# A graph network's convolution loop: ten products with a zero matrix in each group of edges

## Chip, cores and metric

One core of a Trainium2 chip runs the whole kernel in one launch. The metric is the device time of that launch in microseconds (us); ten runs of the kernel before give a median of 4104.05 us (4099.78 to 4107.27).

TensorE (PE in the profile) does the matrix products, VectorE (DVE) and ScalarE (ACT) the elementwise work, GpSimd (POOL) issues the indirect gathers, SyncE (SP) the plain transfers. PEld is TensorE's loading of the stationary matrix, which overlaps its products. "Granted clock" is the share of TensorE's full clock that the throttle let through.

## What is computed

Two graph layers on 6250 nodes of 128 features and 200000 edges sorted by destination. The first (graph attention, two passes) fills the first half of the time and is not touched. The second is a convolution over edges, and the change lies in its loop:

```python
h = jnp.maximum(_layernorm(x), 0.0)
f0, f1 = x0 @ W_lin0_feat, einsum('nui,uv->nvi', x1, W_lin1_feat)   # of h, per node
e0, e1 = f0[edge_src], f1[edge_src]                                  # gathered per edge
a0, a1 = edge_attr[:, 0], edge_attr[:, 1:4]
h = gelu(gelu(edge_scalar_attr @ W_mlp1) @ W_mlp2)                   # 8 -> 64 -> 64 per edge
w = einsum('pxu,ex->epu', W_tp, h)                                   # 4 x 32 weights per edge
m0 = w[:, 0] * e0 * a0
m1 = w[:, 3] * einsum('eui,ei->eu', e1, a1)
m2 = w[:, 1] * e0 * a1
m3 = w[:, 2] * e1 * a0
agg = zeros.at[edge_dst].add(concat(m0, m1, m2, m3))                 # 256 sums per node
out = COS_MIX * self_part + SIN_MIX * (agg @ Wf)
x = x + out
```

(The constant scales are left out here.)

## The kernel before

**Tiles and groups.** The 200000 edges are 1563 tiles of 128 edges (an edge per partition). The loop over `groups` in the convolution takes eight tiles at a time (`SB` = 8): 196 groups, the last one of three tiles. Destinations are sorted, so 24 consecutive tiles (`CT` = 24, three groups) fall on a window of 128 nodes; these three groups are a *chunk*, and 66 chunks make up the loop. I call three consecutive groups a *cycle*.

**One open sum per chunk.** `state["acc"]` is a PSUM tile of 128 nodes x 512 columns (256 sums, each as a high and a low half in fp32r). It is `whole()`, a pool with one buffer. For each tile `scatter` (L1552) multiplies a one-hot matrix of destinations (`ohr`) by the messages (`halves`), 128 x 512, and adds it to that sum. `sink` (L1590 to L1601) says which matmul starts and which stops the accumulation: tile 0 and tile 23 of a chunk. At tile 6 it also adds what of the preceding chunk lies in this one's nodes (L1600). When a new chunk begins, `close` (L1582) copies the sum out on ACT, and `finish3` turns it into output rows in two steps, which are handed over to the two groups after it (`todo`): first transposes of the copy (L1560, eight matmuls) and a copy `at` (L1562), then products with the output weights (L1565, L1566) and the copy `o` (L1568).

**Work of a group, spread over three groups ahead.** While the messages of group g are made, the gather (L351, eight indirect DMAs on POOL) fetches the source rows of group g+1 into one of six `G` buffers, and ACT scales them into `g0` (L1494, eight activations). `layers(g+3)` is a generator with four steps for the edge network of group g+3: first matmul (L1475, from `a8t`), first GELU (L1478), second matmul (L1475, from `hid`), second GELU (L1478). Both of its matmuls write the one PSUM buffer `layer`. `weigh` (L1487) makes the weights `w` of group g+2 in a `big()` buffer, of which there are two.

**Messages on DVE** (`messages`, L1497 to L1542): L1507, L1509 and L1511 read the gathered `G`; then come the two halves of the `mess` part: L1518, L1519, a cast on ACT (L1527, L1532) and the residual of that cast (L1524); L1535 the other part, cast on ACT by L1537, with its residual L1541. L1541 is the last reader of the `big` buffer. L1545 makes the one-hots of the next group.

**Order.** `keep` fixes the order of each engine's instructions as the program writes them. On TensorE, a group issues: first matmul of g+3; a step of `finish3` if one is due, and then the second matmul at once; `weigh` of g+2; the second matmul if no step was due; the eight matmuls of `scatter`. On ACT: L1527, L1532, L1537; the second GELU if it was not yet issued (`between`); eight times L1494; the first GELU; `at` or `o`, or at a chunk's first group the copy of `close`; the second GELU at once if a step of `finish3` was due. So in a cycle there are three kinds of group:

- the *closing* group (the first of a chunk), which copies the old sum; its second GELU comes late, behind the next L1537 on ACT;
- the *transposing* group after it, whose first matmul has to wait for that late GELU (both use `layer`), and which then issues L1560;
- the *output* group, which issues L1565 and L1566.

In the transposing and the output group the second GELU stands in front of the next group's L1527 on ACT.

Of the kernel before, what the change touches and what calls it, by code (L numbers as in the profile page):

```python
# [32 lines left out]
BF16 = mybir.dt.bfloat16  # L33
# [10 lines left out]
P = 128  # L44
# [4 lines left out]
WSTEP = 16  # L49
HS = 7  # L50
CT, LT = 24, 40
DENSE1 = 20
LAG_D, AFTER, AFTER_D = 14, 12, 5
GP, GK, GSB = 125, 16, 4
# [9 lines left out]
def gnn_kernel(ctx: ExitStack, tc: tile.TileContext, x, src, dst, attr4, attr8,  # L64
# [3 lines left out]
    nc = tc.nc  # L68
# [24 lines left out]
    NT = src_t.shape[1]  # L93
    NG = NB - DENSE1
    HALF = P // 2
# [16 lines left out]
    keep = tc.keep_in_program_order  # L112

    def big():
        return ps_big.tile([P, 8, P], F32, tag="big", name="big")
# [10 lines left out]
    def whole():  # L126
        return ps_acc.tile([P, 512], F32, tag="acc", name="whole")
# [391 lines left out]
    def flags(pool, *why):  # L519

        flag = pool.tile([1, NB + 1], F32, name="flag")
        nc.vector.tensor_copy(flag[:, :NB], why[0])
        for w in why[1:]:
            nc.vector.tensor_tensor(flag[:, :NB], flag[:, :NB], w, op=OP.max)
        nc.vector.tensor_reduce(flag[:, NB:], flag[:, :NB], axis=AX.X, op=OP.max)
        flag_i = pool.tile([1, NB + 1], I32, name="flag_i")
        nc.vector.tensor_copy(flag_i, flag)
        return flag_i[:, :NB], flag_i[:, NB:]
# [146 lines left out]
    keep = lambda ins: ins  # L675
# [79 lines left out]
    rhs1 = [dram.tile([P, NB, HW], BF16, name=f"rhs1{q}") for q in range(H1 // 2)]  # L755
    deg1 = pool.tile([P, DENSE1], F32, name="deg1")

# [185 lines left out]
    def miscounted(pool, deg, edges, n):  # L943


        many = pool.tile([P, n], F32, name=f"many{n}")
        nc.vector.tensor_scalar(many, deg, 256.0, None, op0=OP.is_gt)
        ps = small()
        nc.tensor.matmul(ps[:1, :n], ones, deg, start=True, stop=True)
        nc.tensor.matmul(ps[:1, P:P + n], ones, many, start=True, stop=True)  # L950
        miss = pool.tile([1, n], F32, name=f"miss{n}")
        nc.vector.tensor_tensor(miss, ps[:1, :n], edges, op=OP.subtract)
        nc.vector.tensor_tensor(miss, miss, ps[:1, P:P + n], op=OP.subtract)
        nc.vector.tensor_scalar(miss, miss, -0.5, None, op0=OP.is_lt)
        return miss

    HH = H1 // 2 * C1
    assert DENSE1 % 4 == 0
    passes = [(b0, q) for b0 in range(NG, NB, 4) for q in range(H1 // 2)]
# [173 lines left out]
    def chunk_of(g):  # L1133
        return (g * SB + HT // 2) // HT

    def first_of(c):
        return max(0, HT * c - HT // 2)

    def last_of(c):
        return HT * c + HT // 2  # L1140
# [13 lines left out]
    def scatter(g, tiles):  # L1154
        c = chunk_of(g)
        if tiles[0] == 0 and g * SB == first_of(c):
            kept1["acc"] = whole()[:, :2 * (HD + H1)]
        for t in tiles:
            nc.tensor.matmul(kept1["acc"], ohs[g][:, t, :], mss[g][:, t].rearrange("e s f -> e (s f)"),  # L1159
                             start=g * SB + t == first_of(c), stop=g * SB + t + 1 == last_of(c))  # L1160
# [36 lines left out]
    for now in range(NGR * MS + MS):  # L1197
# [35 lines left out]
        if g and m >= 2:  # L1233
            scatter(g - 1, ((0, 1), (2, 3), (4,), (5,), (6,), (7,))[m - 2])
# [12 lines left out]
    keep = plain  # L1247
    nc.vector.tensor_scalar(wtp_sb[:, 0:3, :], wtp_sb[:, 0:3, :], 1.0 / math.sqrt(HID), None, op0=OP.mult)
    nc.vector.tensor_scalar(wtp_sb[:, 3, :], wtp_sb[:, 3, :], 1.0 / math.sqrt(3.0 * HID), None, op0=OP.mult)
    written_order.close()  # L1250
    nc.vector.tensor_tensor(over1[:, NG:], over1[:, NG:], miscounted(pool, deg1, n_edges[:, NG:], DENSE1), op=OP.max)
    again, some = flags(pool, over1, wide1.to_broadcast([1, NB]))
# [58 lines left out]
    with tc.tile_pool(name="att2", bufs=1) as pool, tc.tile_pool(name="dense", bufs=2) as dense, \  # L1311
# [68 lines left out]
        for b0 in range(0, NB, 2):  # L1380
            n = min(2, NB - b0)
# [10 lines left out]
            acc = big().rearrange("p (k a) c -> p k (a c)", k=2)  # L1392
            if b0 == 8:
                load_tiles(pool)
            for h0 in range(0, NB, HS):
# [15 lines left out]
                for j, made in ((0, up), (1, down)):  # L1411
                    for h in range(HS):
                        for k in range(n):
                            nc.tensor.matmul(acc[:, k, j * C2:(j + 1) * C2], made[:, h, k * P:(k + 1) * P],
                                             rhs2[:, h0 + h, j, :],
                                             start=h0 + h + j == 0, stop=h0 + h + j == NB)
                next(behind, None)
            parts = dense.tile([P, 2, 2, R2], F32, name="parts")
            acc = acc[:, :n, :2 * C2].rearrange("p k (j c) -> p k j c", j=2)
# [30 lines left out]
    cw = ctx.enter_context(tc.tile_pool(name="cw", bufs=2))  # L1450
# [31 lines left out]
    def weigh(n, hid, pw):  # L1482

        for j in range(min(n, NPR)):
            for c in range(j, n, NPR):
                half = slice(c // NPR * HID, (c // NPR + 1) * HID)
                keep(nc.tensor.matmul(pw[:, c, :], hid[half, j * P:(j + 1) * P],  # L1487
                           wtp_sb[half].rearrange("x p u -> x (p u)"), start=True, stop=True))
        return pw
# [54 lines left out]
    def one_hot3(dl, n, oh):  # L1544
        keep(nc.vector.tensor_tensor(oh[:, :n, :], slot[:, None, :].to_broadcast([P, n, P]),  # L1545
                          dl[:, :, None].to_broadcast([P, n, P]), op=OP.is_equal))
        return oh

    def scatter(ms, oh, cs, sink):
        for c in cs:  # L1550
            acc, start, stop = sink(c)
            keep(nc.tensor.matmul(acc, oh[:, c, :], ms[:, c].rearrange("e s h i u -> e (s h i u)"), start=start, stop=stop))  # L1552
# [19 lines left out]
    with tc.tile_pool(name="conv", bufs=1) as pool, tc.tile_pool(name="gath3", bufs=6) as gath:  # L1572
# [4 lines left out]
        state, todo = {}, deque()  # L1577

        def close(c):

            a = cw.tile([P, 2, 2 * D], F32, name="acc3")
            keep(nc.scalar.copy(a.rearrange("p s f -> p (s f)"), state["acc"]))  # L1582
            state["sums"] = [a[:, j] for j in range(2)]
            xb = cw.tile([P, D], F32, name="xb")
            nc.sync.dma_start(xb, xtd[ds(first_node(c), P), :])
            ending = finish3(state["sums"], xb, out[ds(first_node(c), P), :])
            next(ending)
            todo.extend([ending, ending])

        def sink(t):  # L1590
            c, k = divmod(t, CT)
            end = min(CT, NT - c * CT) - 1
            if k == 0:
                state["acc"] = whole()
            if k == min(6, end) and c:

                same = cw.tile([P, P], F32, name="same")
                keep(nc.vector.tensor_scalar(same, slot, shift[:, c - 1:c], None, op0=OP.is_equal))
                for a in state["sums"]:
                    keep(nc.tensor.matmul(state["acc"][:, :2 * D], same, a, start=False, stop=False))  # L1600
            return state["acc"], k == 0, k == end  # L1601

        groups = [(t, min(SB, NT - t)) for t in range(0, NT, SB)]

        def hots(g):
            t, n = groups[g]
            return one_hot3(dstc[:, t:t + n], n, cw.tile([P, SB, P], F32R, name="ohr", bufs=3))

        def layers(g):
            if g >= len(groups):  # L1610
                return iter(())
            t, n = groups[g]
            a8t = cw.tile([2 * NRAD, NPR * P], F32, name="a8t", bufs=4)
            for j in range(2 if n > NPR else 1):
                c = (t + j * NPR) * P
                nc.sync.dma_start(a8t[j * NRAD:(j + 1) * NRAD, :], attr8_t[:, c:c + NPR * P])
            return hidden(n, a8t)
# [8 lines left out]
        def keep_a1(t):  # L1626
            m = min(LT, NT - t)
            a1s = kept[:, P + t // LT % 2 * 3 * LT:P + (t // LT % 2 + 1) * 3 * LT].rearrange("p (k f) -> p k f", f=3)
            keep(nc.vector.tensor_copy(a1s[:, :m], a4s[t][:, :m, 1:]))
            return a1s  # L1630

        def fetch(g):
            t, n = groups[g]
            if t % LT == 0 and t + LT < NT:
                load_a4(t + LT)
            G = gath.tile([P, SB, D], F32, tag="G", name="G")
            gather(G, table3, srcc[:, t:t + n], n)
            return G, scaled(G, n, a4s[t // LT * LT][:, t % LT:t % LT + n, 0:1])
# [13 lines left out]
        for g, (t, n) in enumerate(groups):  # L1652
            G, g0 = rows
            i = t % LT
            last = g + 1 == len(groups)
            ms, after = messages(G, g0, n, a1s[:, i:i + n, :], pws.popleft(), None if last else lambda: hots(g + 1),
                                 lambda: hids.extend(list(second)[-1:]))
            if i + SB == LT and t + SB < NT:
                a1s = keep_a1(t + SB)
            first = layers(g + 3)  # L1660
            next(first, None)
            if not last:
                rows = fetch(g + 1)
            next(first, None)
            pw = big() if hids or todo else None
            if todo:
                todo.popleft().send(pw)
                next(first, None)
            if t and t % CT == 0:
                close(t // CT - 1)  # L1670
            if hids:
                pws.append(weigh(groups[g + 2][1], hids.popleft(), pw))
            next(first, None)
            scatter(ms, oh, range(n), lambda c: sink(t + c))
            second = first
            oh = after
# [118 lines left out]
```

## Time and profile before

| | |
|---|---|
| median of ten runs | 4104.05 us |
| the profiled execution | 4104.88 us, its span 4103.1 us |
| first and last gather of the convolution | 2125.2 us, 4078.9 us |
| TensorE busy in 2125 to 4075 us | 1481.63 of 1950 us, granted clock 0.84 |
| DVE busy there | 1746.55 us |
| ACT busy there | 1145.92 us |
| POOL busy there | 1474.56 us |
| mean granted clock of the whole span | 0.815 |

The convolution takes the second half of the span. A busy share does not tell which engine sets the pace: POOL's share counts only the gathers themselves, not the time between two of them in which it issues the next; TensorE's includes stretches at half clock. What ends each wait, in order of time, has to be read from the waits and the timeline.

### The profile page before, as it was taken

How to read it: one execution, taken by the hardware profiler on the slowest of the kernel's cores; microseconds unless marked ns; L12 is line 12 of the kernel's file. 1: busy time of each engine (PE TensorE's matmuls, PEld its weight loads, DVE VectorE, ACT ScalarE, POOL GpSimd, SP SyncE). 2: the span in 40 equal slices, each digit the busy share in tenths (PEclk: the TensorE clock that was granted, in tenths of full speed). 3: DMA queues.
4: the chain of work that ended last, by engine and by line, in shares of the span. 5: the costliest groups of instructions: out<-in, count | busy, mean ns of one | idle time of the engine just before them, and what ended most of it. 6: DMA issues, size and time to landing. Idle time of an engine off the chain costs nothing. (4 is left out here: it accounts for less than half of the span.)

```text
span 4103.1 us, 61327 instructions
## 1 busy us (share of the span) xinstructions
PE 2975.8 (73%) x19231; PEld 2091.8 (51%) x19232; DVE 3590.2 (87%) x6074; ACT 2793.1 (68%) x6317; POOL 2648.8 (65%) x2568
## 2 busy tenths in 40 slices
PE   3456676666666766999977777777777777777777
PEld 3344454444444546888854444444444444444444
DVE  6888988998988877899969989999998898988997
ACT  3458878887877776999965655655555555555555
POOL 5778877777877770000027777777777777777775
PEclk7557868887877777999978888888888888888888
DMA  4456656666666665544422222222222222222221
GB/s 120 146 166 186 192 166 178 190 185 180 179 176 174 183 171 189 182 163 168 166 70 61 63 62 63 62 63 63 62 63 62 64 62 62 63 62 63 62 62 49
DMA packets 391299, 482.40 MB, mean 118 GB/s; under 512 B 237609, under 2 KB 273300, under 8 KB 390950
## 3 DMA queue, kind: packets, MB, share of 16 engines
q1 hardware_dynamic: 307780, 332.00, 25.9%
q0 software_dynamic: 82400, 144.35, 13.5%
q8 instruction: 159, 2.61, 0.3%
q10 hardware_dynamic: 770, 1.88, 0.2%
q14 instruction: 190, 1.56, 0.1%
HBM read 374.52 MB, written 103.42 MB: 116 GB/s over the span
## 5 line engine op out<-in xcount | busy, mean ns | idle before, releaser
L351 POOL DMA_INDIRECT G<-table,srcc x1563 | 1478.3, 946 | 1019.4 <-DVE kept L1458 543.0
L351 POOL DMA_INDIRECT G<-table,srcw x936 | 1105.8, 1181 | 293.4 <-issue 270.3
L1095 ACT ACTIVATE up<-erb,sel 128x512 bf16<-128x512 f32 x980 | 689.4, 733 | 0.0
L877 PE MATMUL small<-key,lo 128*128 128x98 bf16 x3136 | 335.3, 241 | 256.7 <-ACT ca L859 233.0
L1552 PE MATMUL whole<-halves,ohr 128*128 128x512 f32 x1563 | 500.9, 458 | 0.7 <-ACT acc L1582 0.7
L1494 ACT ACTIVATE g<-G,a 128x128 f32<-128x128 f32 x1563 | 485.1, 393 | 12.4 <-DMA G<-table,srcc 9.8
L859 ACT CAST ca<-small 128x392 bf16<-128x392 f32 x784 | 381.0, 489 | 152.9 <-DMA counts<-ca 90.1
L1010 PE MATMUL up<-up,rc 128*102 128x512 bf16 x980 | 434.4, 464 | 47.7 <-DVE up L1019 23.2
L1401 ACT ACTIVATE ramp<-erb,sel 128x256 bf16<-128x256 f32 (+1 forms) x1138 | 458.3, 493 | 13.9 <-DVE up L1409 8.8
L1487 PEld LDWEIGHTS big<-wtp_sb,hid 64*128 64x128 f32 x3126 | 264.7, 250 | 370.7 <-issue 358.1
L877 PEld LDWEIGHTS <-lo 128*128 128x128 bf16 x3136 | 244.7, 117 | 366.1 <-issue 333.1
L1487 PE MATMUL big<-wtp_sb,hid 64*128 64x128 f32 x3126 | 306.5, 351 | 144.9 <-DVE halves L1541 144.4
L1552 PEld LDWEIGHTS whole<-halves,ohr 128*128 128x128 f32 x1563 | 313.3, 207 | 129.1 <-issue 53.9
L1159 PE MATMUL whole<-halves,ohr 128*128 128x136 f32 x936 | 365.2, 443 | 9.7 <-DVE ring L1167 9.7
L1478 ACT ACTIVATE hid<-layer 128x512 f32<-128x512 f32 x392 | 230.7, 589 | 198.9 <-PE layer L1475 198.9
L1475 PE MATMUL layer<-hid,wm_sb 128*128 128x512 f32 x392 | 347.7, 986 | 16.8 <-ACT hid L1478 15.0
L1475 PE MATMUL layer<-a8t,wm_sb 16*128 16x512 f32 x392 | 229.3, 666 | 153.2 <-ACT hid L1478 143.9
L1532 ACT CAST halves<-mess 128x512 fp32r<-128x512 f32 x195 | 114.4, 587 | 330.1 <-DVE mess L1519 330.1
L1524 DVE TENSOR_TENSOR halves<-mess,halves 128x512 fp32r<-128x512 f32 x391 | 268.1, 686 | 57.4 <-ACT halves L1527 41.7
L1019 DVE TENSOR_TENSOR up<-up,ctc 128x3584 bf16<-128x3584 bf16 x140 | 282.5, 2018 | 27.2 <-ACT up L1095 16.0
L1537 ACT CAST halves<-big 128x1024 fp32r<-128x1024 f32 x196 | 197.8, 1009 | 80.1 <-DVE big L1535 80.1
L1159 PEld LDWEIGHTS whole<-halves,ohr 128*128 128x128 f32 x936 | 221.2, 254 | 55.4 <-issue 25.6
(306 smaller groups left out, 6322.3 us busy)
## 6 DMA issues: line engine op xcount, KB each, us to landing
counts<-ca SPq DMA_DIRECT2D x196, 392.0 KB
ct<-counts SPq DMA_DIRECT2D x196, 392.0 KB
ctc<-counts SPq DMA_DIRECT2D x1120, 56.0 KB
oht<-dlow SPq DMA_DIRECT2D x58, 512.0 KB
rc<-rhs SPq DMA_DIRECT2D x70, 358.8 KB
G<-table,srcc POOLq DMA_INDIRECT x1563
G<-table,srcw POOLq DMA_INDIRECT x936
a8t<-attr_rows SPq DMA_DIRECT2D x391, 16.0 KB
```

What stands on the lines that cost most here:

```text
L351: nc.gpsimd.indirect_dma_start(out=G[:, c, :], out_offset=None, in_=table, in_offset=bass.IndirectOffsetOnAxis(ap=idx[:, c:c + 1], axis=0))
L859: nc.scalar.copy(ca[:, :, k * W:(k + WBANK) * W].rearrange("p h (k d) -> p h k d", d=W), ps[:, :WBANK * NKEY].rearrange("p (k h d) -> p h ...
L877: nc.tensor.matmul(ps[:, n * NKEY:(n + 1) * NKEY], lo[:, a, :, r], ky[:, a, :, r], start=True, stop=True)
L1010: nc.tensor.matmul(sums["ups"][j][:2 * C1, :], r[:, i, c:c + 2 * C1], up[:, i], start=h0 + i == 0, stop=h0 + i == NB - 1)
L1019: nc.vector.tensor_tensor(by_part, by_part, state["ct", p, h0].rearrange("p k a h d -> p h (k a) d"), op=OP.min)
L1095: nc.scalar.activation(up[:, i], state["erb", p][:, j], AF.Relu, bias=sel1[:, h0 + i, 2 * q + j:2 * q + j + 1], scale=STEEP)
L1159: nc.tensor.matmul(kept1["acc"], ohs[g][:, t, :], mss[g][:, t].rearrange("e s f -> e (s f)"), start=g * SB + t == first_of(c), stop=g * SB ...
L1401: nc.scalar.activation(ramp[:, h, :n * P], erb[:, :n * P], AF.Relu, bias=sel2[:, h0 + h, :], scale=STEEP)
L1475: keep(nc.tensor.matmul(ph, w, x[:, :npr * P], start=True, stop=True))
L1487: keep(nc.tensor.matmul(pw[:, c, :], hid[half, j * P:(j + 1) * P], wtp_sb[half].rearrange("x p u -> x (p u)"), start=True, stop=True))
L1494: keep(nc.scalar.activation(g0[:, c], G[:, c, :], AF.Copy, scale=a0[:, c, :]))
L1552: keep(nc.tensor.matmul(acc, oh[:, c, :], ms[:, c].rearrange("e s h i u -> e (s h i u)"), start=start, stop=stop))
```

## The change

A zero matrix `nothing` of 128 x 128 in bf16 is made once, ahead of the loop. In each group but the first, ten matmuls with it as the stationary matrix, and its first column broadcast to 512 columns as the moving one, are added to the open sum `state["acc"]`. They add zero. They stand, in program order, behind the first matmul of `layers(g+3)`, the gather of group g+1 and the first GELU, and before `big()`, the step of `finish3`, `weigh` and `scatter`. As TensorE keeps that order, they run between the first matmul and whatever comes next. At a chunk's first group they go to the old chunk's sum and the last of them now carries its stop flag, which tile 23 carried before; the very last chunk, of three tiles, still stops at its last tile. `close` copies the sum behind them. Nothing is taken away: 195 groups get 1950 matmuls more.

```diff
+BUSY = 10
...
+    nothing = cw.tile([P, P], BF16, name="nothing", bufs=1)
+    nc.vector.memset(nothing, 0.0)
+
+    def busy(acc, n, stop):
+
+        for i in range(n):
+            keep(nc.tensor.matmul(acc, nothing, nothing[:, 0:1].to_broadcast([P, 4 * P]),
+                                  start=False, stop=stop and i == n - 1))
+
...
-            return state["acc"], k == 0, k == end
+            return state["acc"], k == 0, t + 1 == NT
...
             if not last:
                 rows = fetch(g + 1)
             next(first, None)
+            if t:
+                busy(state["acc"], BUSY, t % CT == 0)
             pw = big() if hids or todo else None
             if todo:
                 todo.popleft().send(pw)
```

## Prediction

> **What bounds the kernel now.** I read the page first, then the waits of the convolution (2150 to 4050 us, 190 groups, that is 63.3 cycles of three), then the timeline of one cycle, then the granted clock in windows of a microsecond.
>
> ```profile
> PEclk7557868887877777999978888888888888888888
> ...
> L351 POOL DMA_INDIRECT G<-table,srcc x1563 | 1478.3, 946 | 1019.4 <-DVE kept L1458 543.0
> ```
>
> The clock is not full in the second half, so there is something to raise. But the gathers set the pace. In the timeline they come like a metronome:
>
> ```profile
> 3502.35 0.94 POOL L351 DMA_INDIRECT G<-table,srcc  x1 [0.30 <-issue]
> 3503.60 0.95 POOL L351 DMA_INDIRECT G<-table,srcc  x1 [0.30 <-issue]
> ...
> 3505.76 1.12 PE L1475 MATMUL layer<-a8t,wm_sb 16*128 16x512 f32 x2 [3.19 <-ACT hid L1478]
> ...
> 3507.17 2.05 PE L1560 MATMUL big<-ident,acc 128*128 128x128 f32 x8 [0.28 <-DVE halves L1541]
> 3507.49 0.95 DVE L1507 TENSOR_TENSOR dot<-G,kept 128x768 f32<-128x768 f32 x1 [0.47 <-issue]
> ...
> 3509.01 1.60 PE L1475 MATMUL layer<-hid,wm_sb 128*128 128x512 f32 x2
> ...
> 3510.65 0.60 ACT L1478 ACTIVATE hid<-layer 128x512 f32<-128x512 f32 x1 [1.02 <-PE layer L1475]
> ...
> 3511.14 0.58 ACT L1527 CAST halves<-mess 128x512 fp32r<-128x512 f32 x1
> ...
> 3511.75 0.69 DVE L1524 TENSOR_TENSOR halves<-mess,halves 128x512 fp32r<-128x512 f32 x1 [0.50 <-ACT halves L1527]
> ```
>
> A gather starts every 1.25 us: 0.95 busy and 0.30 until the next. No POOL wait in the whole window is longer than 0.3 us, so POOL is never held up by buffers; 1562 steps lie between 2125.2 and 4078.9 us, 1.251 us each. Eight make 10.0 us per group, 30.0 us per cycle. DVE follows: at L1507 it waits for the gather (0.47 us here), its sign that POOL is ahead of nothing. The same lines show TensorE's one path to the end: in the transposing group the first matmul (3505.76), the transposes, the second matmul, the second GELU, the cast L1527 and DVE's L1524, which waited 0.50 us for it.
>
> ```profile
> DVE dot L1507 <- issue: 52.0, 107, 1.1
> DVE halves L1524 <- ACT halves L1527: 40.0, 80, 1.8
> DVE dot L1507 <- DVE kept L1629: 8.8, 16, 0.9
> DVE halves L1524 <- PE big L1487: 3.4, 6, 1.2
> ```
>
> Columns: total wait, times, longest. At L1507 DVE waits 52.0 + 8.8 = 60.8 us, 0.96 per cycle: this is the slack behind POOL. At L1524 it already loses 43.4 us, 0.69 per cycle. So DVE can lose 0.96 + 0.69 = 1.65 us per cycle at L1524 before it, and not POOL, sets the pace.
>
> ```profile
> 3506.00:3507.00 1.00, 0.88 (x2) 0.05 (x1) 1.00 (x1) 1.00 (x4) 0.90 (x1) 0.88 0.25 66
> 3507.00:3508.00 1.00, 0.83 (x4) 0.86 (x5) 0.54 (x2) 1.00 (x5) 0.69 (x2) 0.50 0.22 61
> 3508.00:3509.00 1.00, 1.00 (x6) 1.00 (x6) 0.97 (x2) 0.51 (x2) 0.69 (x2) 0.50 0.15 45
> 3509.00:3510.00 1.00, 1.00 (x3) 0.34 (x2) 1.00 (x3) 0.37 (x1) 0.69 (x2) 0.50 0.23 66
> 3510.00:3511.00 1.00, 1.00 (x10) 0.46 (x10) 0.79 (x3) 0.35 (x1) 0.80 (x1) 0.92 0.21 66
> ```
>
> The third number from the right is the granted clock. After TensorE's idle 3.19 us before 3505.76 the clock halves, not at once but about 1 us into the chain, and for 3.4 us. In quarter-microsecond windows over the whole stage I count 159 such low stretches, 134 of about 3.4 us and 22 of twice that. In 55 of 65 transposing groups one lies near the chain; it begins 0.3 to 3.7 us after the first matmul.
>
> **The change, part by part.**
>
> *The memset* of `nothing`: one DVE instruction before the loop, where DVE sits idle 5.72 us before L1458. Nothing; uncovered it would be some tenths of a microsecond.
>
> *The ten matmuls' own length.* No row has this shape. Nearest in pace are the bf16 runs of L1414, at full clock:
>
> ```profile
> 2087.43 1.34 PE L1414 MATMUL big<-rhs,down 128*128 128x196 bf16 x14
> 2088.61 1.34 PE L1414 MATMUL big<-rhs,up 128*128 128x196 bf16 x14
> ```
>
> 14 x 196 columns take 1.18 us from start to start, 0.43 ns a column, so 512 columns take 0.22 us and ten 2.2 us; 4.4 us at half clock. The other end is L1010's 128x512 bf16 record, 380 ns median, 3.8 us for ten if ends did not overlap. I take 2.2, since L1414's are back to back as these will be. Loads of the stationary matrix (122 to 126 ns in L1010's rows) hide behind 220 ns of product.
>
> *Where they are covered.* TensorE was idle 1950 − 1481.6 = 468 us in the window, 2.4 us per group. In the closing and output groups it waits 1.8 to 2.6 us for L1541 just where the ten stand; what sticks out there, up to 0.6 us, is in front of `weigh` (needed a group later) or of the second matmul of the output group, whose GELU has little to lose (all L1524 waits there sum to 13.9 us in the stage). `close` is behind the first GELU on ACT (in the cycle at 3016 us the old copy starts at 3017.77, the wait for L1541 ends at 3016.8), so the moved stop costs nothing in the steady loop. If this cover is gone, L1524 waits as in the next paragraph.
>
> *Where they are not.* In the transposing group there is no such gap: the first matmul comes late, and L1560 starts 1.41 us after it, 0.28 of which is idle. Chain from the first matmul at full clock, from rows: 1.12 (first matmul) + 2.2 + 1.05 (L1560, eight, at 4093.61 us) + 1.12 (second matmul, as at 3017.92 us), less 0.2 at each of three joints, because the next record starts before the last one ends = 4.9 us. It was 4.85 here (3510.61 − 3505.76), at half clock for most of it. From the second GELU to L1524 are 1.10 us, so L1524 can start 6.0 us after the first matmul. DVE alone would be there at 5.99 − 0.50 − 0.47 = 5.0 us. Wait: 1.0 us per cycle, below 1.65. At full clock it would cost nothing.
>
> *The clock.* The gap before this chain is not filled: TensorE waits there for the late GELU, and the ten come behind it. With the group before running faster, the gap is rather 3.5 us each time than 1.6 to 3.5 as now. So the low stretch comes again, and now the chain has no idle time in it to swallow it: 3.4 us at half clock do 1.7 us of work, the chain takes 6.6, and the wait becomes 2.7 us. Bounds: 1.0 (never low) and 4.4 (twice as long, all inside the chain). I take the counts of now: 10/65 at 1.0 and 55/65 at 2.7, mean 2.44, and 14% (22 of 159) double, +1.7 each, 0.24: 2.7 in all. Excess over the slack 2.7 − 1.65 = 1.05 us per cycle, times 65: **+68 us**.
>
> The trace halves the clock after gaps of 1.6 us too (in the cycle at 2306 us TensorE idles 1.63 us before the first matmul, and the clock is low 2.1 us later). A rule speaks against this step: the Trainium skill ("TensorE: Matmul & The Clock Gate", on the HAM clock gate and "Why this matters for your kernels") has the clock halve only after about one idle window of 3.4 us and asks to avoid gaps over some 3 us. By the rule the gap of 3.2 to 3.5 us would hardly fill a window, the clock would stay full and the excess be zero; by the rows it is as summed above.
>
> *The tail.* In group 195 the ten stand behind the scatter that ends at 4091.3 us, and `close` (4091.32) waits for them, with all that follows: 2.2 to 4.4 us, less some gain from the clock. I take 3.
>
> Sum: 68 + 3 = 71 us on the profiled execution's 4104.88 (span 4103.1 and 1.8 around it), which is 0.8 above the median; on the median: **4175 us**.
>
> **Rivals.**
>
> *No change.* The ten keep the clock up through the chain, or the low stretch falls behind it; the wait stays under 1.65 and POOL's 10.0 us still rule. For it: the threshold lies between gaps that I know only as they are now, and 10 of 65 chains have no low stretch. Against: the longest gap stays. Time 4104 + 0 to 4 us.
>
> *Much slower.* Zeros don't count for the clock, so the change does not do what it is to do, and low stretches last two windows: wait 4.4, excess 2.75 x 65 = 179, 4104 + 179 + 4 = 4287 us. Against: nothing in the trace tells zeros from data.
>
> *Faster.* POOL's 0.30 us between gathers is in part a hidden wait on DVE's buffers; then the 43.4 us lost at L1524 (45 in 65 cycles) come back once the chain is ahead of L1527: 4059 us. It decides where the spacing of gathers falls below 1.25 us. Against: 941/947/962 ns and 0.30 between, the same while the six buffers are first filled.
>
> **Numbers.** Forecast 0.60, no change 0.23, much slower 0.10, faster 0.07. The forecast's own range is 4135 to 4225 (wait 2.1 to 3.4 per cycle). The range of 8 in 10 reaches down over no change: 4102 to 4225. Faster by over 0.2% (8.2 us, what a measurement of this kernel can tell) 0.07, within 0.2% 0.23, slower 0.70.
>
> **What would show it.** Right: gathers further apart than 1.25 us on average, or with waits over 0.3; the wait at L1507 near zero, that at L1524 some 150 us or more, in transposing groups; L1560 starting some 3 us after the first matmul; half clock inside that chain, and less of it elsewhere; stage clock above 0.84. Wrong: L1507 still waiting for gathers at a spacing of 1.25 (no change), or the ten at another pace than 0.22 us, or no low stretch after the 3.5 us gap.

## The result, and the profile after

The changed kernel takes 4196.61 us (median of 8 runs, 4191.76 to 4205.76) against 4103.75 us for the kernel before in the same session: a ratio of 1.0228, 95% interval 1.0219 to 1.0237, 93 us slower. The profiled execution has a span of 4197.9 us.

From the page of the changed kernel (its source has moved: L351 is now L352, L1475 L1476, L1478 L1479, L1507 L1508, L1524 L1525, L1527 L1528, L1552 L1562, L1560 L1570, L1562 L1572, L1582 L1592; the ten are L1556); columns as before, the last ones being busy us, mean ns, and idle time ahead with its releaser:

```profile
PEclk7557878887787868999979999999999999999999
...
L352 POOL DMA_INDIRECT G<-table,srcc x1563 | 1474.8, 944 | 1069.5 <-DVE kept L1459 542.8
...
L1556 PE MATMUL whole<-nothing 128*128 128x512 bf16 x1950 | 562.7, 445 | 0.0
...
L1525 DVE TENSOR_TENSOR halves<-mess,halves 128x512 fp32r<-128x512 f32 x391 | 268.0, 685 | 223.5 <-ACT halves L1528 190.5
```

The clock did what the change is for: 0.93 in 2125 to 4075 us, against 0.84 before. The time went to the last line: DVE's idle before the mess residual (L1525, which takes the rounding rest of the cast L1528). The waits of the loop (2150 to 4140 us, again 190 groups) say who is late now:

```profile
POOL G L352 <- issue: 403.3, 1315, 1.6
...
DVE halves L1525 <- ACT halves L1528: 185.9, 57, 4.7
...
POOL G L352 <- ACT hid L1479: 61.2, 43, 3.4
...
DVE halves L1525 <- ACT hid L1479: 15.2, 5, 3.0
```

Two things have changed places. DVE no longer waits for a gather anywhere: no line of L1508 is left. And POOL, which never waited over 0.3 us, now does, up to 3.4 us at a time: its six buffers are full, because DVE is behind. (The releaser L1479 is only the last one that the profile saw: 35 of POOL's 38 pauses over 0.35 us end 0.74 us after DVE's last read, L1512, of the gathered rows of the group six before, which lie in the same buffer.) The gathers are 1.281 us apart on average, 1.251 before. Before, gathers set the pace; now the loop through DVE, ACT and TensorE does.

The timeline of one transposing group shows where (3036.97 is the late second GELU of the closing group):

```profile
3036.97 0.60 ACT L1479 ACTIVATE hid<-layer 128x512 f32<-128x512 f32 x1
...
3037.63 1.12 PE L1476 MATMUL layer<-a8t,wm_sb 16*128 16x512 f32 x2 [3.62 <-ACT hid L1479]
...
3038.68 4.02 PE L1556 MATMUL whole<-nothing 128*128 128x512 bf16 x10
...
3042.54 1.05 PE L1570 MATMUL big<-ident,acc 128*128 128x128 f32 x8
...
3043.43 1.02 PE L1476 MATMUL layer<-hid,wm_sb 128*128 128x512 f32 x2
...
3044.49 0.60 ACT L1479 ACTIVATE hid<-layer 128x512 f32<-128x512 f32 x1 [0.49 <-PE layer L1476]
...
3044.99 0.58 ACT L1528 CAST halves<-mess 128x512 fp32r<-128x512 f32 x1
...
3045.60 0.69 DVE L1525 TENSOR_TENSOR halves<-mess,halves 128x512 fp32r<-128x512 f32 x1 [3.04 <-ACT halves L1528]
```

And the granted clock there (third number from the right):

```profile
3037.00:3038.00 1.00, 0.37 (x1) 0.29 (x2) 1.00 (x3) 1.00 (x4) 0.70 (x2) 1.00 0.15 41
3038.00:3039.00 1.00, 1.00 (x4) 0.20 (x3) 1.00 (x2) 1.00 (x5) 0.69 (x2) 1.00 0.09 25
3039.00:3040.00 1.00, 1.00 (x5) 0.32 (x4) 0.97 (x2) 1.00 (x5) 0.69 (x2) 0.56 0.29 82
3040.00:3041.00 1.00, 1.00 (x4) 0.43 (x3) 1.00 (x2) 0.38 (x1) 0.90 (x1) 0.50 0.31 82
3041.00:3042.00 1.00, 1.00 (x4) 0.29 (x2) 0.90 (x3) 0.00 (x0) 0.80 (x1) 0.50 0.21 66
3042.00:3043.00 1.00, 1.00 (x7) 0.79 (x6) 0.46 (x2) 0.00 (x0) 0.69 (x2) 0.74 0.18 53
```

TensorE idles 3.62 us, starts the chain at full clock, and the clock halves 1.5 us after the chain's start, among the first of the ten. They take 4.02 us here and 2.35 us where the clock is full. The chain from the first matmul to the end of the second is 6.82 us (3044.45 − 3037.63), L1525 waits 3.04 us for it.

### The profile page after: what moved, and what is told of

The parts are those of the page before. It is cut to its first block, busy times and chain, and to the rows that moved or that the text cites. A ratio compares the mean times of both kernels' runs of the same rounds, so it can differ in the third digit from the quotient of the medians.

```text
span 4197.9 us, 65228 instructions
## 1 busy us (share of the span) xinstructions
PE 3252.7 (77%) x21181; PEld 2153.0 (51%) x21182; DVE 3579.1 (85%) x6075; ACT 2791.1 (66%) x6317; POOL 2645.8 (63%) x2568
## 5 line engine op out<-in xcount | busy, mean ns | idle before, releaser
L352 POOL DMA_INDIRECT G<-table,srcc x1563 | 1474.8, 944 | 1069.5 <-DVE kept L1459 542.8
L352 POOL DMA_INDIRECT G<-table,srcw x936 | 1105.9, 1182 | 290.0 <-issue 270.9
L1556 PE MATMUL whole<-nothing 128*128 128x512 bf16 x1950 | 562.7, 445 | 0.0
L1562 PE MATMUL whole<-halves,ohr 128*128 128x512 f32 x1563 | 458.7, 429 | 0.7 <-ACT acc L1592 0.7
L1525 DVE TENSOR_TENSOR halves<-mess,halves 128x512 fp32r<-128x512 f32 x391 | 268.0, 685 | 223.5 <-ACT halves L1528 190.5
L1556 PEld LDWEIGHTS <-nothing 128*128 128x128 bf16 x1950 | 197.6, 109 | 414.5 <-issue 279.3
L1476 PE MATMUL layer<-a8t,wm_sb 16*128 16x512 f32 x392 | 237.0, 686 | 221.7 <-ACT hid L1479 212.6
L1562 PEld LDWEIGHTS whole<-halves,ohr 128*128 128x128 f32 x1563 | 286.0, 189 | 98.6 <-issue 17.5
L1479 ACT ACTIVATE hid<-layer 128x512 f32<-128x512 f32 x392 | 230.6, 588 | 99.4 <-PE layer L1476 99.3
L1488 PEld LDWEIGHTS big<-wtp_sb,hid 64*128 64x128 f32 x3126 | 195.1, 190 | 182.1 <-PE whole L1556 62.6
L1488 PE MATMUL big<-wtp_sb,hid 64*128 64x128 f32 x3126 | 230.9, 287 | 52.2 <-DVE halves L1542 51.7
```

The costliest lines, as they stand in the source:

```text
L352: nc.gpsimd.indirect_dma_start(out=G[:, c, :], out_offset=None, in_=table, in_offset=bass.IndirectOffsetOnAxis(ap=idx[:, c:c + 1], axis=0))
L1525: keep(nc.vector.tensor_tensor(ms[:, cs, 1, 1], m, ms[:, cs, 0, 1], op=OP.subtract))
L1556: keep(nc.tensor.matmul(acc, nothing, nothing[:, 0:1].to_broadcast([P, 4 * P]), start=False, stop=stop and i == n - 1))
```

## The experiments

The theory: the ten cost time only in the transposing group, by making the chain first matmul, ten, transposes, second matmul, second GELU, cast longer than the slack that DVE has behind the gathers; the half clock in that chain does the larger part. Rivals: the ten cost the same wherever they stand; the length alone is enough; the gathers have hidden slack and a better clock pays.

On one of the two chips that the experiments fell on, the kernel before took 5242 us; no trace of it was kept there. In the traces of the other kernels from that chip engines stand still for long: between 2700 and 4900 us ACT is idle for over 4 us at a time, 17 to 106 times in a trace and up to 18.8 us, mostly before a GELU and with "remote" as the releaser, and the engines that need it wait behind it. One of the texts below says that every engine stopped; the traces show otherwise, the gathers go on until their buffers are full. The cause is not known. The first and the last four runs were made on that chip and can't answer for the 4104 us kernel.

### The first four: where the ten stand

```diff
# not in the transposing group
-            if t:
+            if t and len(todo) != 2:
                 busy(state["acc"], BUSY, t % CT == 0)
# in the transposing group alone, stop back at k == end
-            if t:
-                busy(state["acc"], BUSY, t % CT == 0)
+            if len(todo) == 2:
+                busy(state["acc"], BUSY, False)
# ahead: the ten before the first matmul
+            if t:
+                busy(state["acc"], BUSY, t % CT == 0)
             first = layers(g + 3)
             next(first, None)
...
-            if t:
-                busy(state["acc"], BUSY, t % CT == 0)
# both: as the changed kernel, and ten more ahead in the transposing group
+            if len(todo) == 2:
+                busy(state["acc"], BUSY, False)
             first = layers(g + 3)
```

`len(todo) == 2` holds in the transposing group only: both steps of `finish3` are still to come.

Not in the transposing group: 

> The ten are left out of the transposing groups (65 of 195) and stay in the closing and output groups. If the whole loss comes from the chain first matmul, ten, transposes, second matmul, second GELU, cast, then DVE waits at the mess residual as before (0.5 us per cycle of three groups, not 3.3), waits for gathers again, and the time is 4104 to 4112 us (the tail of the last group costs some 2 to 5). If the ten cost the same wherever they stand (a load on TensorE, on PSUM or on the clock), two thirds of the 93 us stay: about 4166 us.

In it alone: 

> The ten stand in the transposing groups alone, the stop flag is back at the last tile of a chunk. If the chain is the cause: the whole loss is there with a third of the matmuls, 4185 to 4205 us; more if the group before it now runs at half clock more often, less if its idle gap is shorter for that reason. If the load is the cause: one third of 93, about 4135 us.

Ahead: 

> All 1950 matmuls stay, but stand before the first matmul of the group and so, in the transposing group, in the idle 3.2 to 3.5 us ahead of the chain instead of inside it. If the chain is the cause and the gathers set the pace: granted clock of the loop above 0.9, the chain is 3.9 to 4.8 us long, the gathers again 1.25 us apart, and the time 4100 to 4108 us: no gain in spite of the better clock. If the gathers have hidden slack, the better clock shows: about 4060 us. If the ten cost wherever they stand: 4190 us or more.

Both: 

> As the changed kernel, and ten more in front of the first matmul of each transposing group: the chain is as long as in the changed kernel, but the idle gap before it is filled by 2.2 us. This tells the length of the chain from its half clock. If the half clock (1.7 us and more per chain) is what pushes it over the slack of about 1.7 us per cycle: the chain takes 4.9 to 5.3 us, the wait is 1.0 to 1.4 us per cycle, and the time goes back to 4104 to 4112 us with 650 matmuls more. If the length alone is enough: 4180 us or more. In between (4130 to 4170) if the gap that remains still lowers the clock in a part of the chains.

Measured against the kernel before on that chip: 0.9878 (0.9805 to 0.9952), 1.0161 (1.0096 to 1.0226), 0.9874 (0.9791 to 0.9957), 1.0126 (1.0055 to 1.0196). None of the expected times can be compared: between 2700 and 5000 us the gathers stood 1.65 to 1.72 us apart on average, with 116 to 142 pauses of over 0.35 us in 1340 to 1389 of them, where the kernel before at 4104 us has none. Inconclusive, so all four were run again.

### The same four again

> The kernel of e1_not_transposing once more: there every engine stopped for some 5 to 15 us in each group or so, in the kernel before too (5242 us), so that neither the gathers nor the chain set the pace. Where the kernel before takes 4104 us again: 4104 to 4112 us if the chain of the transposing group is the whole cause, about 4166 us if the ten cost the same everywhere.

> The kernel of e2_only_transposing once more. 4185 to 4205 us if the chain is the cause, about 4135 us if the ten cost the same everywhere.

> The kernel of e3_ahead once more. Chain cause and the gathers as floor: 4100 to 4108 us, chain 3.9 to 4.8 us, granted clock of the loop above 0.9; about 4060 us if the gathers have hidden slack; 4190 us or more if the ten cost wherever they stand.

> The kernel of e4_both once more. 4104 to 4112 us with a chain of 4.9 to 5.3 us if the half clock is needed to push the chain over the slack; 4180 us or more if the length alone is enough; in between if the rest of the gap still lowers the clock in a part of the chains.

The kernel before took 4107.87 us beside them, which is what the last four ratios stand on; the first two rows are from the session of the result. The columns after the ratio are read from the traces over 61 to 63 cycles (three groups each), as means: what DVE waited per cycle at the mess residual and for gathers, the length of a cycle (by where one cuts it, 0.1 us more or less), the chain from the first matmul's start to the second one's end, TensorE's idle gap ahead of that chain, in how many of 63 chains the clock was at half for a part, and the granted clock in 2125 to 4075 us.

| kernel | time, us | ratio (95%) | residual | gathers | cycle | chain | gap | half clock | clock |
|---|---|---|---|---|---|---|---|---|---|
| before | 4104.05 | | 0.69 | 0.96 | 29.94 | 4.78 | 2.10 | 53 | 0.84 |
| changed | 4196.61 | 1.0228 (1.0219 to 1.0237) | 3.22 | 0 | 31.39 | 7.14 | 3.24 | 62 | 0.93 |
| not transposing | 4107.03 | 1.0003 (0.9993 to 1.0014) | 1.12 | 0.51 | 29.91 | 5.45 | 3.32 | 62 | 0.90 |
| transposing alone | 4185.43 | 1.0191 (1.0158 to 1.0224) | 2.91 | 0 | 30.99 | 6.37 | 2.52 | 41 | 0.87 |
| ahead | 4108.42 | 1.0000 (0.9989 to 1.0010) | 0.19 | 1.28 | 29.92 | 4.19 | 0.76 | 21 | 0.93 |
| both | 4110.87 | 1.0013 (1.0000 to 1.0027) | 1.87 | 0 | 30.03 | 5.74 | 1.07 | 22 | 0.97 |

**Place, not load.** 1300 of the 1950 matmuls cost nothing (1.0003); the other 650 alone cost 1.9%. The rival "the same wherever they stand" asked for 4166 and 4135 us and is out. DVE's waits in the two, first without and then with the ten in the transposing group alone (columns: total, times, longest; 2150 to 4050 us):

```profile
DVE halves L1525 <- ACT halves L1528: 70.4, 60, 2.0
DVE dot L1508 <- issue: 27.7, 65, 0.7
DVE dot L1508 <- DVE kept L1639: 4.5, 10, 0.8
```

```profile
DVE halves L1525 <- ACT halves L1528: 169.9, 98, 4.7
DVE halves L1525 <- PE big L1488: 4.4, 2, 3.0
DVE halves L1525 <- ACT hid L1479: 2.7, 2, 1.4
```

In the first DVE still waits for gathers, at L1508, so POOL sets the pace. In the second that wait is gone, as in the changed kernel.

The two do not add up to the 2.3% of the changed kernel, and the columns on the gap and the half clock say why. The ten in the other groups act on the chain from outside: with them the gap ahead of it is 3.2 to 3.3 us and nearly every chain has half clock, without them 2.1 to 2.5 us, and 53 or 41 chains have it. "Not transposing" shows this alone: its chain has no matmul more than before and is 0.67 us longer, and DVE waits 1.12 us at the residual, not the 0.5 that was expected. It fits into the slack there, so the time stays.

**A better clock with nothing to gain.** "Ahead" has all 1950 matmuls and a clock of 0.93, the shortest chain, and the time of before to 0.1%. Its waits:

```profile
DVE dot L1508 <- issue: 69.3, 135, 1.4
DVE halves L1525 <- ACT halves L1528: 12.2, 28, 1.1
DVE dot L1508 <- DVE kept L1639: 11.6, 21, 1.0
```

Of what DVE no longer loses at L1525 (43.4 us before, 12.2 now) 20 us come back as waits for the gathers (60.8 before, 80.9 now), which stay 1.249 us apart. The rival "hidden slack" asked for 4060 us and is out.

**Length against half clock.** In "both" the chain has the ten in it as in the changed kernel, and ten more in the gap ahead of it. One of its transposing groups:

```profile
3007.21 1.12 PE L1476 MATMUL layer<-a8t,wm_sb 16*128 16x512 f32 x2 [1.42 <-ACT hid L1479]
...
3008.27 2.35 PE L1556 MATMUL whole<-nothing 128*128 128x512 bf16 x10
...
3010.45 1.05 PE L1570 MATMUL big<-ident,acc 128*128 128x128 f32 x8
...
3011.34 1.02 PE L1476 MATMUL layer<-hid,wm_sb 128*128 128x512 f32 x2
...
3012.40 0.60 ACT L1479 ACTIVATE hid<-layer 128x512 f32<-128x512 f32 x1 [0.49 <-PE layer L1476]
3012.90 0.58 ACT L1528 CAST halves<-mess 128x512 fp32r<-128x512 f32 x1
3013.51 0.69 DVE L1525 TENSOR_TENSOR halves<-mess,halves 128x512 fp32r<-128x512 f32 x1 [1.37 <-ACT halves L1528]
```

The wait is 1.37 us here, also the median over the loop, with a median chain of 5.15 us; in the changed kernel these are 3.03 and 6.82. The run also holds both cases side by side: the 41 chains that kept full clock take 5.15 us and DVE waits 1.3 us after them; the 22 with one low stretch take 6.8 us and it waits 2.9 us. (The means, 5.74 and 1.87, lie above the 4.9 to 5.3 and 1.0 to 1.4 that were expected, because of these 22.) With 650 matmuls more than the changed kernel it is 86 us faster and within 0.3% of before. So the length alone is not enough; the half clock in the chain, which comes from the gap ahead of it, is what carries it over the slack. "Both" stands right on the edge: the wait for gathers is 0 and the cycle 30.03 us, which is the gathers' 24 x 1.251. In quarter-microsecond windows I count 25 low stretches of the clock in its loop, where the changed kernel has 66.

### The last four: without the gathers' floor, and five instead of ten

```diff
# in the kernel before, in "ahead" and in the changed kernel
+        Gs = [gath.tile([P, SB, D], F32, name=f"G{i}", bufs=1) for i in range(6)]
+        for i in range(6):
+            nc.vector.memset(Gs[i][:, SB - 1, :], 0.0)
...
-            G = gath.tile([P, SB, D], F32, tag="G", name="G")
-            gather(G, table3, srcc[:, t:t + n], n)
+            G = Gs[g % 6]
+            gather(G, table3, srcc[:, t:t + n], min(n, SB - 1))
# five
-BUSY = 10
+BUSY = 5
```

> The kernel before without the gather of the eighth tile of each group: its rows are zeros set once, so its messages are left out of the sums and the time is that of a loop whose gathers take 8.75 us per group and no longer 10.0. If the gathers set the pace before, the time falls, but only until the other loop rules: DVE's own work of about 28.2 us per cycle plus 1.0 to 1.5 us of waits at the mess residual, 29.2 to 29.7 against 29.9 us now, so 4055 to 4090 us. If the gathers do not set the pace: 4104 us.

> The kernel with the ten ahead of the first matmul, also without the gather of the eighth tile (its messages are left out of the sums). This asks what the better clock is worth where the gathers don't hide it. The chain was 4.2 us there against 4.8 before; with DVE's 28.2 us and 0.2 to 0.6 us of waits per cycle: 28.4 to 28.8 us, 4010 to 4045 us, some 40 us faster than the kernel before without the eighth gather. If the clock is worth nothing even then, the two are equal.

> The changed kernel without the gather of the eighth tile (its messages are left out of the sums). If the chain sets its pace and the gathers no longer do: nothing changes, 4188 to 4200 us. If the gathers still share in it, it falls by 10 us or more.

> The changed kernel with five matmuls instead of ten. Five at 0.22 us, or 0.43 at half clock, shorten the chain of the transposing group by 1.1 to 2.1 us, from 7.1 to 5.0 to 6.0, and the wait from 3.3 to 1.2 to 2.2 us per cycle, about the slack of 1.7 to 1.9. So it breaks even or nearly: 4104 to 4130 us. If each matmul costs its share: 4150 us.

Measured in this order, beside 5247.86 us for the kernel before on that chip: 0.9326 (0.9256 to 0.9397), 0.9653 (0.9584 to 0.9722), 0.9818 (0.9765 to 0.9870) and 1.0094 (1.0055 to 1.0132). The halts fill these traces too: in the run with five, TensorE idles 9.7 us (median) before the first matmul of the chain and the chain then runs low from its start (median 7.7 us, longer than with ten on the other chip). Three answers stay open: what the loop would take without the gathers' floor, what the better clock is worth there, and whether five would break even.

## Why the prediction was right, and where it was off

**The floor.** That the gathers set the pace and that a better clock buys nothing was right, and shown by "ahead": clock 0.93, chain 0.6 us shorter, ratio 1.0000.

**The chain.** The step that decides, ten matmuls in front of L1560 in the transposing group, was right in place (0.0% without it, 1.9% with it alone) and in mechanism: the gap was not filled, it grew as forecast (from 2.1 to 3.24 us on average), and the clock halved inside the chain. Two readings behind it were loose: the gaps of before are not 1.6 to 3.5 us but 0.4 to 3.6 with a median of 1.95, so the cycle that was worked from, with 3.19, lies near the long end; and L1570 starts 5.1 us after the first matmul, not some 3, because the low stretch falls on the ten themselves. The low stretches in the other groups vanished: 159 in the loop before, 66 now, one for each cycle.

**Sizes.** The forecast was 4175 us, the result 4196.61: an excess of 71 against 93. The ten's own length was nearly right (2.35 us as a record at full clock, the last matmul's end included, 2.2 predicted). Three terms were too small:

- The chance of a low stretch. I took over the counts of before: 55 of 65 chains, 14% of them twice as long, which comes to 1.7 us per chain. After, there is one in every cycle, and 17 of 66 (26%) are double; 4.2 us of a chain run low on average, which costs 2.1 us.
- The chain at full clock. It is 5.15 us (the 41 chains of "both" that kept it), where I had 4.9. With 2.1 for the clock this makes 7.2 us; the mean measured is 7.14, where my sum amounts to about 6.6. So the wait was 3.22 us per cycle and not 2.7.
- The slack. It was 1.65 us from the listed waits. From the cycles of the changed kernel DVE's own work is 31.39 − 3.22 = 28.17 us, so against the gathers' 30.0 it is some 1.85 us. "Both" agrees: it stands on the edge with a wait of 1.87 us.

By these the excess per cycle is 3.22 − 1.85 = 1.4 us, times 65 is 89 us, and with the tail it comes near the 93. The cycle lengths alone say 31.39 − 29.94 = 1.45, 94 us. The first two errors and the third pull against each other: with the slack at 1.85 and the wait still at 2.7 the sum would have given 0.85 x 65 = 55 us and not 68. That the forecast came as near as 71 to 93 is in part luck.

**The tail.** Predicted 3 us. In the last group `close` waited 2.49 us for the ten; of the kind expected.

**Cover in the other groups.** Right for the time: without the transposing ones the ten cost 0.03%, within the error. That they lengthen the chain of the transposing group from outside is in the gap and the chance above. The moved stop flag is in that run too, so it costs nothing that can be seen.

**The rivals.** "No change" needed the clock to stay up through the chain, and "both" shows that this is indeed the condition: there it does in 41 of 63 chains, and the time is within 0.3% of before. "Much slower" needed zeros not to count for the clock; the clock rose to 0.93 and 0.97 on zeros. "Faster" fell with "ahead". The Trainium skill ("TensorE: Matmul & The Clock Gate", on the HAM clock gate and "Why this matters for your kernels") asks for no idle gaps over some 3 us, and gives one idle window, of about 3.4 us, as what brings the half clock. The gaps of 3.24 us in the changed kernel are over the first figure and under the second, and they brought a low stretch in each cycle; in the kernel before, where half of the gaps are under 2 us, 53 of 63 chains had one. So the rows were the better guide.

## What to carry to other kernels

Work that is added to keep a clock up belongs into the idle gap itself, ahead of the latency chain that follows it; in this kernel the same ten matmuls cost nothing before the chain's first instruction and 2.3% behind it. Before paying for a faster engine, look at which engine never waits: here POOL with its gathers, which came no closer than 1.25 us apart at any clock from 0.84 to 0.97. An engine that is idle a quarter of the time can still have one stretch per cycle with no room in it, so cover has to be read stretch by stretch, not from the mean of 2.4 us per group.

## What was not expected of the hardware

The clock changes only on a fixed grid. In each of the six traces of the table every change of the granted clock in the convolution lies on a grid of 3.413 us, to within 0.01 us. Cut the loop into windows on that grid: of the windows at full clock in which TensorE's rows leave 60% or more idle, 278 of 278 were followed by half clock; of those with under 20% idle, 0 of 1804; in between, 211 of 662. So the cost of a gap falls on what runs in the window after the one that holds it. In the kernel before none of the transposing chains was low at the first matmul, 11% were 0.5 us later and 80% 3.5 us later, after gaps of 0.4 to 3.6 us; in "not transposing" half of the chains were low already at the first matmul; in the changed kernel the ten themselves are hit. Why some stretches last two windows the idle shares do not tell.

And products of a zero matrix count as work for the clock: with 1950 of them 0.93 was granted where it had been 0.84, and 0.97 in "both" with 2600. No run has the same matmuls on other data.
